# Collecting a mixture of experts' rows: block 0 summed by TensorE, the other tiles by VectorE alone, tables cleared at the start

## The chip, the cores and the metric

One core of one Trainium2 chip runs the whole program: a network of four layers on 4096 tokens of 128 features, float32 throughout. The metric is the device time of one run, in microseconds (us). A run of the kernel before takes 4406.22 us (median of three: 4403.34, 4406.22, 4411.11).

The engines by the names of the profile: PE is TensorE (matrix products), PEld its weight loads, DVE is VectorE, ACT is ScalarE, POOL is GpSimd, SP is SyncE, which only issues DMAs here. "L1742" is line 1742 of the kernel.

## The reference, cut to what matters

Each layer is a feed-forward, an attention, and the same feed-forward again. The change is in layer 3's feed-forward, which runs twice: before layer 3's attention and after it, as the last stage of the program. It is a mixture of 64 experts of which each token takes 8, with 64 places per expert, and one shared expert:

```python
probs = softmax(x @ router_w.T)
topk_w, topk_ids = top_k(probs, 8)            # 8 experts of 64 per token
topk_w = topk_w / sum(topk_w)
pos = place of the token among those that chose the expert, in token order
valid = pos < 64                              # C = 64 places per expert
y = (silu(xb @ w_gate) * (xb @ w_up)) @ w_down     # per expert, 64 rows each
routed = segment_sum(y[its 8 places] * weight * valid, token)
shared = silu(x @ ws_gate) * (x @ ws_up) @ ws_down
x = x + 0.5 * (routed + shared)               # on layernorm(x) as input
```

Places are given in token order over all 4096 tokens, so 64 experts with 64 places take 4096 of the 32768 choices: the first ones. Tokens late in the order get nothing from the experts.

## The kernel before

**Tiling.** x stays on chip as 32 tiles of 128 tokens; four tiles are a block (8 blocks). Tile and block lie in `self.X`; `self.XT` holds the normalized blocks with features on the partitions. A tile framework schedules the instructions of each engine from a model when the program is built, places the buffers of pools in memory, and inserts semaphore waits; each engine then executes its own list in order. DMAs stand in the list of the engine that issues them (SP, ACT or POOL) and wait there.

**Routing** (`ffn3`, L1709; `route`, L1744). `SOON = 3`: first only blocks 0 to 2 are routed. Per block, `stats` issues two DMAs that write zeros to 1 MB each of `parts` in DRAM (`clear`, L1738, issued by ACT at L1742; six in all) and takes the layer norm's moments, whose power -0.5 POOL forms (L168); `norm` scales (L175); `turn` transposes the block on PE (L185) and ACT copies it to XT (L187); `logits` multiplies (L1762) and DVE forms maximum (L1768) and difference (L1770), ACT the exponential (L1771); `choose` normalizes (L1777 to L1779), takes the eight largest (L1783, L1784), writes the row with its weights to `table` in DRAM (L1794, SP) and makes keys (L1800 to L1807). Five steps of three blocks are staggered (`route_blocks`, L1821). The keys are transposed (L1818, L1819), each expert's first 64 tokens are picked by eight rounds of "eight largest" (`choose_tokens`, L1843, L1845), and `places` makes a list of rows to fetch and of rows of `parts` to write. If some expert still has room, `more` is 1 and blocks 3 to 7 are routed too (`If`, L1892). In the profiled run `more` is 0: only 24 collecting reads (two times 12) are in the trace.

**Experts** (L1957). Eight groups of eight experts: POOL fetches the tokens' rows by indirect DMAs (L1951), PE multiplies, DVE weights the results, POOL scatters them by indirect DMAs to `parts` (L1988), where each token has eight rows of 128 numbers, one per chosen expert, zero where it got no place. The shared expert (L1912 to L1930) is interleaved.

**Collecting** (L2009 to L2029). For each of the 12 tiles of blocks 0 to 2: SP reads its eight rows per token, 512 KB, from `parts` (L2012, six buffers `co`); POOL adds the upper four rows to the lower four (128 partitions x 512, L2017); DVE halves the rest twice (128x256, L2018; 128x128, L2019) and adds half of the sum to x (L2021). Then `If(more)` (L2027) does the same for the other 20 tiles. An `If` is a branch on every engine; its other arm on SP waits until the DMA semaphores have reached the counts that they should have there, and adds what the skipped DMAs would have added. In the last call each block is stored by ACT when its four tiles are done (L2032).

**What follows the first call**: `attention3` (L804). It opens a pool, clears two value buffers V of 128x2048 (L827, POOL) and two of maxima (L831, POOL), normalizes block 0 (L164, L165, L167 on DVE, L168 on POOL, L175 on DVE), transposes it on PE (L975), copies it by ACT (L976) and forms queries and keys (L847, L849, L855, L857). L895 and L901 are its products and their maxima.

**The start of the program** (`ready2`, L2043): a zero tile `blank`; SP writes zeros with it to `table` (L2057, L2058), to `table2` for layer 2 (L2063, 16 DMAs of 1 MB) and to parts of `rel_rows` of layer 0's attention (L393).

## Time and profile before

| what | us |
|---|---|
| median of three runs | 4406.22 |
| the profiled execution | 4419.59 |
| its span, first to last instruction | 4417.8 |
| first routing, until the first fetch | 3437.7 to 3499.6 |
| first collecting, first read to the last sum | 3589.30 to 3621.77 |
| layer 3's attention, first scaling | 3622.38 |
| second routing, until the first fetch | 4230.7 to 4288.73 |
| second collecting, first read to the last sum | 4386.40 to 4413.49 |

| engine | busy us | share of the span |
|---|---|---|
| PE | 3785.8 | 86% |
| PEld | 2065.0 | 47% |
| DVE | 2765.6 | 63% |
| ACT | 2086.6 | 47% |
| POOL | 980.7 | 22% |

How to read it. The timeline gives instructions in order of start: start us, duration us, engine, line, operation, out<-in, count; in square brackets the engine's idle time before it and what ended it. "ACTq" or "SPq" is the issuing of a DMA in that engine's list, "POOLq" a wait there. The stretches give, for a part of the span, each engine's busy time with its number of instructions, the TensorE clock granted (1.00 is full speed), the share of the DMA engines' time and GB/s.

### The profile page before, as it was taken

The page shows a single profiled execution, that of the slowest core. Times are in us where ns is not written, and L with a number is a line of the kernel's source. Part 1 is how long each engine was busy: PE and PEld are TensorE (multiplying, and loading weights), DVE is VectorE, ACT ScalarE, POOL GpSimd, SP SyncE. Part 2 cuts the span into 40 slices and gives each one's busy share as a digit, 9 for nine tenths or more (in the row PEclk, how much of TensorE's full clock was granted, in tenths as well). Part 3 has the DMA queues.
Part 4 walks back from the last instruction along what each step waited for, and adds up shares of the span by engine and source line. Part 5 has one row for each costly group of instructions (what it writes and reads, how often), then busy time and mean ns, then how long its engine had stood idle before and what let it go on. Part 6 is the DMA issues. An engine that isn't in the chain of part 4 may idle for free. (4 is left out here: it accounts for less than half of the span.)

```text
span 4417.8 us, 64316 instructions
## 1 busy us (share of the span) xinstructions
PE 3785.8 (86%) x23046; PEld 2065.0 (47%) x23046; DVE 2765.6 (63%) x7495; ACT 2086.6 (47%) x4422; POOL 980.7 (22%) x1270
## 2 busy tenths in 40 slices
PE   8999999999999868899999967868667359999946
PEld 3445666666544345434344444467347233333324
DVE  5655777777756566656656466656553556777654
ACT  2335877878533324377877623312213015555521
POOL 1001111111000265211111266143024350000026
PEclk9999999999999979989999979969668579999967
DMA  6006777777300000000000000035007430000035
GB/s 256 0 5 203 220 226 221 223 221 225 93 1 1 5 0 1 1 1 1 1 1 1 1 0 2 8 100 172 0 13 239 153 125 1 1 1 1 1 109 169
DMA packets 217613, 331.79 MB, mean 75 GB/s; under 512 B 19954, under 2 KB 188380, under 8 KB 213700
## 3 DMA queue, kind: packets, MB, share of 16 engines
q1 hardware_dynamic: 197284, 290.59, 20.5%
q0 software_dynamic: 9664, 19.84, 1.5%
q10 hardware_dynamic: 10336, 17.17, 1.0%
q8 instruction: 183, 3.00, 0.3%
q14 instruction: 146, 1.20, 0.1%
HBM read 182.71 MB, written 144.82 MB: 74 GB/s over the span
## 5 line engine op out<-in xcount | busy, mean ns | idle before, releaser
L509 DVE CUSTOM_DVE_ANT_0 ps_s<-ps_s,PB 128x512 f32<-128x512 f32 x512 | 352.3, 704 | 155.5 <-PE ps_s L501 73.8
L901 DVE TENSOR_REDUCE nm<-ps_one 128x1 f32<-128x512 f32 x512 | 328.9, 685 | 155.4 <-PE ps_one L895 140.3
L513 ACT ACTIVATE pn<-ps_s,nm 128x512 f32<-128x512 f32 x512 | 356.8, 697 | 104.8 <-DVE nm L509 104.8
L907 ACT ACTIVATE pt<-ps_one 128x512 f32<-128x512 f32 x512 | 277.6, 595 | 203.7 <-PE ps_one L895 157.8
L168 POOL TENSOR_TENSOR ln_rs<-ln_rs,mhalf 128x4 f32<-128x4 f32 x128 | 132.7, 1037 | 897.5 <-DVE ln_rs L167 887.4
L895 PE MATMUL ps_one<-KT,QT 32*128 32x512 f32 x1024 | 307.5, 662 | 0.8 <-ACT KT L857 0.8
L675 ACT ACTIVATE sc<-sc,nm 128x512 f32<-128x512 f32 (+3 forms) x512 | 285.8, 562 | 39.5 <-DVE nm L732 33.3
L525 PE MATMUL ps_one<-ident,pn 128*128 128x128 f32 x2048 | 293.3, 282 | 12.2 <-DVE y L562 9.8
L732 DVE CUSTOM_DVE_ANT_0 sc<-ps_one,mask 128x512 f32<-128x512 f32 (+3 forms) x512 | 232.3, 487 | 105.5 <-PE ps_one L723 86.3
L887 PE MATMUL ps_one<-Q,KT 32*128 32x512 f32 x1024 | 289.7, 639 | 0.0
L326 ACT ACTIVATE sg<-ps_big 128x512 f32<-128x512 f32 x224 | 132.3, 597 | 320.2 <-PE ps_big L324 300.0
L450 PE MATMUL ps_one<-rdiff,QT 32*128 32x256 f32 x940 | 267.4, 404 | 14.5 <-ACT pt L528 14.4
L525 PEld LDWEIGHTS ps_one<-ident,pn 128*128 128x128 f32 x2048 | 219.1, 141 | 122.2 <-ACT pn L513 37.4
L327 DVE TENSOR_TENSOR sg<-sg,ps_big 128x512 f32<-128x512 f32 x224 | 152.3, 684 | 194.1 <-ACT sg L326 192.4
L739 ACT ACTIVATE pt<-ps_one 128x512 f32<-128x512 f32 (+3 forms) x512 | 209.6, 431 | 101.0 <-PE ps_one L723 92.9
L323 PE MATMUL ps_big<-XT,slot_a 128*128 128x512 f32 x448 | 236.7, 610 | 12.2 <-DVE sg L327 12.2
L501 PE MATMUL ps_s<-KT,QT 32*128 32x512 f32 (+2 forms) x1024 | 237.3, 540 | 0.8 <-ACT E L454 0.7
L324 PE MATMUL ps_big<-XT,slot_a 128*128 128x512 f32 x448 | 233.2, 602 | 0.0
L723 PE MATMUL ps_one<-KT,QT 32*128 32x512 f32 (+3 forms) x1024 | 229.7, 494 | 3.5 <-ACT pt L739 2.8
L715 PE MATMUL ps_one<-Q,KT 32*128 32x512 f32 (+3 forms) x1024 | 226.2, 483 | 6.8 <-ACT KT L662 5.8
L335 PE MATMUL ps_acc<-h,slot_a 128*128 128x512 f32 x448 | 229.8, 596 | 0.4 <-DVE h L329 0.4
L456 POOL COPY E<-E 128x127 f32<-128x127 f32 (+1 forms) x256 | 88.6, 346 | 637.2 <-ACT E L454 631.5
(436 smaller groups left out, 8386.1 us busy)
## 6 DMA issues: line engine op xcount, KB each, us to landing
rel_rows<-E SPq DMA_DIRECT2D x192, 383.0 KB, 3.7
PB<-rel_rows SPq DMA_DIRECT2D x128, 384.0 KB, 3.4
wt<-in_f_w_dram SPq DMA_DIRECT2D x78, 512.0 KB, 4.2
PB<-rel_rows SPq DMA_DIRECT2D x128, 256.0 KB
table<-blank SPq DMA_DIRECT2D x16, 1032.0 KB, 17.8
rel_rows<-E SPq DMA_DIRECT2D x64, 256.0 KB, 3.2
parts<-zero ACTq DMA_DIRECT2D x12, 1024.0 KB, 11.7
co<-parts SPq DMA_DIRECT2D x24, 512.0 KB, 7.1
```

Source lines behind the costliest of these rows:

```text
L323: nc.tensor.matmul(out=gu[:, 0, :], lhsT=w["f0_g"][:, cs], rhs=self.XT[:, b, :], start=True, stop=True)
L324: nc.tensor.matmul(out=gu[:, 1, :], lhsT=w["f0_u"][:, cs], rhs=self.XT[:, b, :], start=True, stop=True)
L450: nc.tensor.matmul(out=ps[:, c * 256 : c * 256 + 256], lhsT=Q[u][rr, i * P : (i + 1) * P], rhs=rdiff[rr, :], start=True, stop=True, tile_p ...
L501: nc.tensor.matmul(out=s[:, k, far:BT], lhsT=qt[rr, i * P : (i + 1) * P], rhs=kt[rr, far:BT], start=True, stop=True, tile_position=(32 * g ...
L509: nc.vector.tensor_tensor_reduce(out=s[:, k, :], in0=s[:, k, :], in1=pb[:, k, PB_AT[i] : PB_AT[i] + BT], scale=-1.0, scalar=1e30, op0=ALU. ...
L513: nc.scalar.activation(pn[:, k, :], s[:, k, :], AF.Exp, bias=nm[:, k : k + 1], scale=-1.0)
L525: nc.tensor.transpose(ps[:, j * P : (j + 1) * P], pn[:, k, j * P : (j + 1) * P], self.ident)
L675: nc.scalar.activation(sc[:, k, 0:wd], sc[:, k, 0:wd], AF.Exp, bias=maxs[u % 2][:, i, g, HD : HD + 1], scale=-1.0, accum_out=SUMS[u][:, i, ...
L887: nc.tensor.matmul(out=tw[k], lhsT=K[uw][rr, j * P : (j + 1) * P], rhs=Q2[uw][rr, :], start=True, stop=True, tile_position=(32 * g, 0),)
L895: nc.tensor.matmul(out=ts[k], lhsT=Q[u][rr, i * P : (i + 1) * P], rhs=K[u][rr, :], start=True, stop=True, tile_position=(32 * g, 0),)
L901: nc.vector.tensor_reduce(maxs[u % 2][:, i, 2 * hp + k : 2 * hp + k + 1, HD], ts[k], AX.X, ALU.max, negate=True)
L907: nc.scalar.activation(PT[m][:, k, :], tw[k], AF.Exp)
```

## The change

- `parts` is no longer one buffer, taken in each call and cleared there, but two buffers, one for each call, taken in `ready2`. The zeros of blocks 0 to 2 of both are written there by 12 DMAs of 1 MB on SP's queue, between those of `table` and those of `table2`. `clear(b)` remains for blocks 3 to 7 only.
- The collecting pool `f3c` is opened with `side="right"`.
- For a tile, DVE makes all three halvings (128x512, 128x256, 128x128); POOL does nothing.
- Block 0 is collected as a whole: four reads into one buffer `co4`, eight matmuls of 128x512 with the identity as weights that accumulate in PSUM, the k-th over row k of each of the 512 tokens, and one DVE instruction 128x512 that adds half of it to x.
- The order is now `If(more)`, block 0, tiles 4 to 11; before it was tiles 0 to 11, `If(more)`.

```diff
             table = self.table
-            parts = self.dram.tile([ROWS + NTOK, D], F32, name="parts", tag="parts", bufs=1)
+            parts = self.parts[last]
...
                 def stats():
-                    clear(b)
+                    if b >= SOON:
+                        clear(b)
                     box["mv"] = self.stats(self.tiles(b))
...
-        with self.tc.tile_pool(name="f3c", bufs=2) as pool:
+        with self.tc.tile_pool(name="f3c", bufs=2, side="right") as pool:
+            def read(dst, t):
+                nc.sync.dma_start(
+                    out=dst, in_=parts[t * P * K3 : (t + 1) * P * K3, :].rearrange("(p j) d -> p (j d)", j=K3)
+                )
+
             def collect(t):
                 c = pool.tile([P, K3, D], F32, name="co", tag="co", bufs=6)
-                nc.sync.dma_start(
-                    out=c.rearrange("p j d -> p (j d)"),
-                    in_=parts[t * P * K3 : (t + 1) * P * K3, :].rearrange("(p j) d -> p (j d)", j=K3),
-                )
+                read(c.rearrange("p j d -> p (j d)"), t)
                 r = pool.tile([P, 4, D], F32, name="cr", tag="cr")
-                nc.gpsimd.tensor_tensor(out=r, in0=c[:, 0:4, :], in1=c[:, 4:8, :], op=ALU.add)
-                nc.vector.tensor_tensor(r[:, 0:2, :], r[:, 0:2, :], r[:, 2:4, :], ALU.add)
-                nc.vector.tensor_tensor(r[:, 0, :], r[:, 0, :], r[:, 1, :], ALU.add)
+                for n in (4, 2, 1):
+                    src = c if n == 4 else r
+                    nc.vector.tensor_tensor(r[:, 0:n, :], src[:, 0:n, :], src[:, n : 2 * n, :], ALU.add)
                 x = self.X[:, t, :]
                 nc.vector.scalar_tensor_tensor(x, r[:, 0, :], 0.5, x, ALU.mult, ALU.add)
...
-            for t in range(4 * SOON):
-                collect(t)
+            def collect_block(b):
+
+                c = pool.tile([P, 4, K3 * D], F32, name="co4", bufs=1)
+                for j in range(4):
+                    read(c[:, j, :], 4 * b + j)
+                ps = self.mid()
+                for k in range(K3):
+                    nc.tensor.matmul(
+                        out=ps.rearrange("p (j d) -> p j d", d=D), lhsT=self.ident,
+                        rhs=c[:, :, k * D : (k + 1) * D], start=(k == 0), stop=(k == K3 - 1),
+                    )
+                x = self.xblk(b).rearrange("p j d -> p (j d)")
+                nc.vector.scalar_tensor_tensor(x, ps, 0.5, x, ALU.mult, ALU.add)
+                if last:
+                    self.store(b)
+
             with self.tc.If(more):
                 for t in range(4 * SOON, NT):
                     collect(t)
+            collect_block(0)
+            for t in range(4, 4 * SOON):
+                collect(t)
...
         nc.sync.dma_start(out=self.table[NTOK : NTOK + 1, :], in_=rows[0:1, 0, :])
+
+        self.parts = [
+            self.dram.tile([9 * NTOK, D], F32, name="parts%d" % n, tag="parts%d" % n, bufs=1) for n in range(2)
+        ]
+        for n in range(2 * self.SOON):
+            for p in self.parts:
+                nc.sync.dma_start(
+                    out=p[n * 16 * P : (n + 1) * 16 * P, :].rearrange("(p k) c -> p (k c)", k=16), in_=zero[:, 0 : 16 * D]
+                )
```

More of the change, by code (lines that the diff above doesn't have):

```diff
@@ L1706, in attn2 @@
                 nc.vector.tensor_tensor(x, x, po, ALU.add)
+    SOON = 3
     def ffn3(self, last):
@@ L1717, in ffn3 @@
         HALF = NTOK // 2
-        SOON = 3
+        SOON = self.SOON
         with self.tc.tile_pool(name="f3", bufs=1) as pool, self.tc.tile_pool(name="f3b", bufs=2) as pool2:
             table = self.table
-            parts = self.dram.tile([ROWS + NTOK, D], F32, name="parts", tag="parts", bufs=1)
+            parts = self.parts[last]
             zero = pool.tile([P, 16 * D], F32, name="zero")
```

## The prediction

> **What bounds the kernel now.** Layer 3's feed-forward runs twice and takes about 317 us of the 4417.8; nothing outside it is edited, except twelve DMA issues at the start. I read first the stretches of both calls (routing, collecting, start of the attention), then the timeline inside each, then the waits, then the order of instructions in the changed program with the semaphores that each waits for.

> The stretches (us; then busy time and instructions of PE, PEld, DVE, ACT, POOL; granted clock; DMA share; GB/s):

> ```profile
> 3430.00:3500.00 70.00, 12.22 (x47) 8.74 (x47) 50.31 (x180) 3.75 (x8) 10.34 (x12) 0.50 0.44 160
> ...
> 3588.00:3622.00 34.00, 0.00 (x0) 0.00 (x0) 24.13 (x56) 0.00 (x0) 17.22 (x14) 0.50 0.50 187
> 3622.00:3660.00 38.00, 33.21 (x78) 11.06 (x82) 23.56 (x55) 3.66 (x6) 7.02 (x8) 0.51 0.00 0
> ```

> Routing and collecting are DVE's: PE does nothing in the collecting. So what counts is when DVE starts, what holds it up, and how fast PE's next work comes free. Routing of the first call:

> ```profile
> 3436.91 0.69 DVE L1612 TENSOR_TENSOR X<-X,yg 128x512 f32<-128x512 f32 x1 [0.80 <-DMA yg<-f_y]
> ...
> 3441.30 0.59 ACT L187 COPY XT<-ps_mid 128x512 f32<-128x512 f32 x1 [22.80 <-PE ps_mid L185]
> 3441.93 10.72 ACTq L1742 DMA_DIRECT2D parts<-zero  x6
> ...
> 3444.87 0.85 DVE L175 TENSOR_SCALAR xw<-X,ln_mv,ln_rs 128x128 f32<-128x128 f32 x3
> 3452.70 0.42 ACT L1771 ACTIVATE p<-p 128x256 f32<-128x256 f32 x1 [10.82 <-DMA parts<-zero]
> 3453.03 0.57 ACT L187 COPY XT<-ps_mid 128x512 f32<-128x512 f32 x1
> 3453.15 0.42 DVE L1777 TENSOR_REDUCE r_s<-p 128x4 f32<-128x256 f32 x1 [7.43 <-ACT p L1771]
> ```

> The reader is to see that six DMA issues stand in ACT's list ahead of block 0's exponential; DVE, ready at 3445.72, waits 7.43 us. In the second call the same six cost DVE 3.51 us (L1777 starts at 4243.24). In the collecting:

> ```profile
> 4399.13 1.32 POOL L2017 TENSOR_TENSOR cr<-co 128x512 f32<-128x512 f32 x1 [0.61 <-DVE X L2021]
> 4399.37 1.23 DVE L2019 TENSOR_TENSOR cr<-cr 128x128 f32<-128x128 f32 x1
> 4400.64 0.29 DVE L2021 SCALAR_TENSOR_TENSOR X<-cr,X 128x128 f32<-128x128 f32 x1
> 4400.85 0.42 DVE L2018 TENSOR_TENSOR cr<-cr 128x256 f32<-128x256 f32 x1
> 4401.06 1.32 POOL L2017 TENSOR_TENSOR cr<-co 128x512 f32<-128x512 f32 x1 [0.61 <-DVE X L2021]
> ```

> A tile takes 1.93 us, and DVE's 128x128 add, 0.29 us alone, lasts 1.23 us while POOL's add runs. Last, the handover to the attention:

> ```profile
> 3621.48 0.29 DVE L2021 SCALAR_TENSOR_TENSOR X<-cr,X 128x128 f32<-128x128 f32 x1
> 3622.11 3.69 POOL L827 MEMSET V<- 128x2048 f32 x2 [2.26 <-DVEq L2027]
> 3622.38 3.57 DVE L175 TENSOR_SCALAR xn<-X,ln_mv,ln_rs 128x128 f32<-128x128 f32 x4 [0.61 <-DVEq L2027]
> ...
> 3626.72 0.58 ACT L976 COPY XT<-ps_one 128x512 f32<-128x512 f32 x1 [45.28 <-PE ps_one L975]
> ```

> **The change, part by part.**

> *Clears out of the calls.* In the changed list ACT does block 0's copy, block 1's copy, then block 0's exponential. First call: block 1's transposes end at 3444.76, its copy about 3445.4, the exponential about 3445.7, so L1777 starts about 3445.75: 7.4 us earlier. DVE's list is also rearranged: block 1's maximum (L1768) is now second, and waits for logits that PE forms from 3445.4 for 1.97 us: a new wait of 1.2 us, with all of DVE's routing queued behind it. The old wait of 0.89 us for block 2's logits shrinks to about 0.1. Net 7.4 - 1.2 + 0.8 = **7.0 us**. Second call: block 0's differences are ready at 4239.73, L1777 moves from 4243.24 to 4240.2, 3.04 - 1.2 + 0.8 = **2.6 us**. From there to the fetches all is DVE work in a row, so the shift arrives whole.

> *Clears at the start.* Twelve issues and 12.6 MB on SP's queue ahead of table2's. The DMA engines are saturated (402 to 422 GB/s) until 78 us, then idle (2 GB/s or less) until the first transfer of layer 0's attention at 329.06 us; 12.6 MB at 410 GB/s is 31 us, ending about 109 us. Everything queued behind on SP shifts by as much: table2 and rel_rows zeros, needed 220 us later. Cost 0; had the cover been gone, 31 us.

> *Collecting, first call.* Let R be the first read's issue (3589.30, last scatter landed); both programs wait for the same scatters. Reads move 408 to 422 GB/s, 1.27 us each. The first is used at R+3.4; by the bytes moved, the fifth lands at R+8.4. In the changed list DVE does tiles 4 to 8, then block 0's addition, then tiles 9 to 11. A tile: the 128x512 add is not in this stage before; L1612 (above, two inputs on chip) takes 0.69. With 0.45, 0.33 and 0.21 between the starts that follow, 1.71 us. It could not beat POOL's 1.93 by more than 0.5, nor be worse than 0.69 replaced by 1.25. PE's eight matmuls: a 128x512 float32 one takes 0.85 between starts at clock 0.50 (L855), so 6.8 us, from R+7 to R+15 with all reads in; hidden, since DVE asks for them only at R+17. Sum: 8.4 + 5 x 1.71 + 0.65 + 3 x 1.6 + 1.1 for the interleaved statistics of the attention = R+23.5; before R+32.5. The 9 us do not all arrive. In the changed program V's clearing waits for DVE's semaphore at the last tile's sum, so the right-hand pool does not free the attention of it, and the power for block 0's norm (L168), which before stood among the collecting additions, now stands behind the clearings in POOL's list: 0.15 + 3.69 + 1.3 for the small ones + 1.03 = R+29.7. Then four scalings of 0.28, a transpose, and the copy (L976) at R+31.5; before R+37.4. Gain **5.9 us**. Were V not held, DVE's statistics would be next and the copy about R+27: 4.5 more.

> *Collecting, second call.* Here the scheduler has put block 0's first read ahead of the `If`, whose other arm on SP waits for that read to land. A read alone: 3.24 us (the chain's first "co<-parts" piece). So the other eleven leave at R+3.9; tile 4, fourth of them, lands at about R+10.9 instead of R+8.4. PE then ends near R+17, still under the tiles. 10.9 + 8 x 1.71 + 0.65 = R+25.3 against R+27.1: gain **1.8 us** (4.3 if the wait cost nothing; -0.5 if the tiles took 2.0 each). The store of the last block stands behind it as before. The `If` was off the tail already (0.61 us on DVE in the first call, beside a store here).

> Sum: 7.0 + 2.6 + 5.9 + 1.8 = 17.3 us. The profiled execution took 4419.59 (4417.8 and 1.8 around it), so that one would be 4402.3; it lay 13.4 above the median of the runs, and I carry the difference to the median: 4406.22 - 17.3 = **4389 us**.

> [...] From 3622 to 3660 PE is busy 33.21 of 38 us, at clock 0.51. [...]

> **Rivals.**

> [...]
> 2. *Slower: half clock for longer.* [...] From 3660 to 4230 PE is busy 562.92 of 570 us, so each us more at half clock costs about 0.5. To end 0.2% above before, it must lose 26 us, 52 us more of it: 4415 and above. Nothing but chance speaks for it.
> 3. *Only the fronts.* Reads land later than by the bytes, or the 128x512 add costs more, and both tails give nothing: 9.6 us, 4396.6. For: 1.71 is put together from rows of other places.
> 4. *Better tails.* V's clearing or the second call's reads hold up less than counted: 7 us more, 4382.
> 5. *It does not do what it says* is in part sure (the pool still holds V) and counted.

> **How the numbers follow.** Forecast 60% (4384 to 4395, its own terms' bounds); rival 1 8%, rival 2 5%, rival 3 15%, rival 4 12%. The range 4379 to 4399 takes in the forecast, 3 and 4. About 0.2%, 8.8 us, is what a measurement can tell from no change, so faster is below 4397.4: 60 + 12 + 8 and half of rival 3, 87%; same 9%; slower 4%.

> **What would show it.** Right: block 0's exponential about 0.4 us after block 1's copy, DVE's wait before block 1's maximum about 1.2 us in both calls; no POOL additions in the collecting and DVE's 128x128 adds at 0.29; block 0's addition waiting for nothing; POOL's power behind the clearings and the copy L976 about 31.5 us after the first read; in the second call a gap of 3 to 4 us on SP between the first and second read. Wrong: DVE idle before tile 5 or later (reads bind), PE's sums later than tile 8, the stretch at half clock much longer or shorter than 36 us, or layer 0's attention starting later than before.

## The result and the profile after

The changed kernel takes 4400.62 us (median of 20 runs, 4390.15 to 4406.53); the kernel before, run beside it, 4408.32 us (20 runs, 4398.92 to 4418.63). The ratio is 0.9979, 95% interval 0.9972 to 0.9986. So it is faster, by 7.7 us between the medians (9.9 between the means), where 17.3 were forecast. Two later pairs, on other chips, gave 0.9973 (0.9959 to 0.9986) and 0.9989 (0.9978 to 0.9999).

The profiled execution of the changed kernel has a span of 4403.2 us against 4417.8: 14.6 less. That is twice the difference of the medians, and it is the riddle of this case. First the stretches of the changed kernel, with the same columns as before the change:

```profile
3430.00:3500.00 70.00, 13.65 (x50) 9.30 (x50) 54.01 (x199) 3.87 (x8) 14.58 (x16) 0.50 0.25 75
...
3588.00:3622.00 34.00, 16.63 (x32) 6.81 (x34) 21.97 (x79) 1.96 (x3) 8.75 (x10) 0.60 0.38 151
3622.00:3660.00 38.00, 38.00 (x143) 12.42 (x137) 24.02 (x41) 10.33 (x17) 0.00 (x0) 0.65 0.00 0
```

Everything has moved forward: PE, idle in the collecting before, now has 16.63 us of work between 3588 and 3622 (the sums of block 0, then the attention's start), and the attention fills the stretch from 3622. The clock column is 0.50 to 0.65. Stretch by stretch, with two traces of each kernel (the second pair is of a chip on which both traces are some 54 us longer: some 42 of it ahead of the attention's first queries, 13 to 14 in the second call's experts, whose rows go by indirect DMAs, and none of it in the stretches of the table):

| stretch, us | before | after | before, 2nd | after, 2nd |
|---|---|---|---|---|
| first routing, first constant (L1731, L1733) to first fetch | 61.90 | 55.52 | 61.62 | 55.50 |
| first collecting, first read to the attention's first copy (L976) | 37.42 | 31.52 | 37.59 | 31.82 |
| attention, that copy to the last addition to X (L960) | 604.6 | 604.6 | 602.1 | 604.7 |
| second routing, first constant to first fetch | 57.48 | 57.06 | 58.03 | 56.92 |
| second collecting, first read to the end of the span | 31.40 | 29.97 | 31.39 | 29.08 |

The four edited stretches give 6.4 + 5.9 + 0.4 + 1.4 = 14.1 us in the first pair and 6.1 + 5.8 + 1.1 + 2.3 = 15.3 in the second. The first front, in the changed kernel's timeline (L1774 is the exponential, L1780 the sum behind it, L1771 a block's maximum):

```profile
3445.79 0.59 ACT L187 COPY XT<-ps_mid 128x512 f32<-128x512 f32 x1 [2.91 <-PE ps_mid L185]
...
3446.47 0.42 ACT L1774 ACTIVATE p<-p 128x256 f32<-128x256 f32 x1
3446.92 0.42 DVE L1780 TENSOR_REDUCE r_s<-p 128x4 f32<-128x256 f32 x1 [0.20 <-ACT p L1774]
```

ACT goes from block 1's copy straight to the exponential, and the sum waits 0.20 us where it waited 7.43. The second front, where little was gained, first two rows of the kernel before, then the changed kernel:

```profile
4243.24 0.42 DVE L1777 TENSOR_REDUCE r_s<-p 128x4 f32<-128x256 f32 x1 [3.51 <-ACT p L1771]
...
4249.24 0.42 DVE L1768 TENSOR_REDUCE r_nm<-ps_mid 128x4 f32<-128x256 f32 x1 [0.89 <-PE ps_mid L1762]
```

```profile
4230.77 0.59 ACT L187 COPY XT<-ps_mid 128x512 f32<-128x512 f32 x1 [2.60 <-PE ps_mid L185]
...
4233.42 0.42 DVE L1771 TENSOR_REDUCE r_nm<-ps_mid 128x4 f32<-128x256 f32 x1 [2.28 <-PE ps_mid L1765]
4233.76 0.34 DVE L1786 MAX8 r_m<-p 128x8 f32<-128x64 f32 x2
```

DVE stands 2.28 us before block 2's maximum, where it stood 0.89; block 0's choice (MAX8) has all it needs, but is queued behind it. Collecting and handover:

```profile
3600.30 0.68 DVE L2024 TENSOR_TENSOR cr<-co 128x512 f32<-128x512 f32 x1
...
3601.02 0.75 DVE L2024 TENSOR_TENSOR cr<-cr 128x256 f32<-128x256 f32 x2
3601.81 0.29 DVE L2026 SCALAR_TENSOR_TENSOR X<-cr,X 128x128 f32<-128x128 f32 x1
3602.02 0.68 DVE L2042 SCALAR_TENSOR_TENSOR X<-ps_mid,X 128x512 f32<-128x512 f32 x1
...
3607.63 3.57 POOL L827 MEMSET V<- 128x2048 f32 x2 [25.83 <-DVE ln_mv L165]
...
3608.03 1.43 DVE L167 TENSOR_SCALAR ln_rs<-ln_mv 128x4 f32<-128x4 f32 x1
...
3612.34 2.02 POOL L168 TENSOR_TENSOR ln_rs<-ln_rs,mhalf 128x4 f32<-128x4 f32 x2
3613.41 1.12 DVE L175 TENSOR_SCALAR xn<-X,ln_mv,ln_rs 128x128 f32<-128x128 f32 x4 [2.19 <-POOL ln_rs L168]
...
3615.15 0.59 ACT L976 COPY XT<-ps_one 128x512 f32<-128x512 f32 x1 [39.74 <-PE ps_one L975]
```

A tile takes 1.72 us (3600.30 to 3602.02), block 0's addition (L2042) waits for nothing (by little, see below), and the norm's power (L168) stands behind the clearings, as forecast.

### The profile page after: what moved, and what is told of

The parts are those of the page before. It is cut to its first block, busy times and chain, and to the rows that moved or that the text cites. A ratio compares the mean times of both kernels' runs of the same rounds, so it can differ in the third digit from the quotient of the medians.

```text
span 4403.2 us, 64326 instructions
## 1 busy us (share of the span) xinstructions
PE 3800.1 (86%) x23078; PEld 2070.6 (47%) x23078; DVE 2748.3 (62%) x7489; ACT 2088.1 (47%) x4422; POOL 952.1 (22%) x1246
## 5 line engine op out<-in xcount | busy, mean ns | idle before, releaser
L168 POOL TENSOR_TENSOR ln_rs<-ln_rs,mhalf 128x4 f32<-128x4 f32 x128 | 132.5, 1036 | 898.9 <-DVE ln_rs L167 888.8
L895 PE MATMUL ps_one<-KT,QT 32*128 32x512 f32 x1024 | 307.9, 663 | 0.8 <-ACT KT L857 0.8
L450 PE MATMUL ps_one<-rdiff,QT 32*128 32x256 f32 x940 | 267.1, 403 | 14.6 <-ACT pt L528 14.5
L525 PEld LDWEIGHTS ps_one<-ident,pn 128*128 128x128 f32 x2048 | 219.0, 141 | 122.5 <-ACT pn L513 37.4
## 6 DMA issues: line engine op xcount, KB each, us to landing
parts<-blank SPq DMA_DIRECT2D x12, 1024.0 KB, 14.1
```

Source lines behind the costliest of these rows:

```text
L450: nc.tensor.matmul(out=ps[:, c * 256 : c * 256 + 256], lhsT=Q[u][rr, i * P : (i + 1) * P], rhs=rdiff[rr, :], start=True, stop=True, tile_p ...
L525: nc.tensor.transpose(ps[:, j * P : (j + 1) * P], pn[:, k, j * P : (j + 1) * P], self.ident)
L895: nc.tensor.matmul(out=ts[k], lhsT=Q[u][rr, i * P : (i + 1) * P], rhs=K[u][rr, :], start=True, stop=True, tile_position=(32 * g, 0),)
```

## The experiments

Each kernel is the changed one with one edit unless said otherwise. "Attention" is always the time from its first copy to the last addition to X.

**1. Second traces, and each half alone.** `clears` is the kernel before with the early clears, `collect` the kernel before with the new collecting.

> The kernel before, unchanged: a second trace of it. The traces of the first pair of executions differ by 14.6 us (4417.8 and 4403.2), the medians by 7.7. Theory A (terms right, this kernel's typical execution has shorter stalls than the profiled one): the first call's wait of VectorE for block 0's exponential, 7.43 us in the first trace, or the collecting (37.4 us from its first read to the attention's first copy) comes out some us shorter here. Theory B (clock): those stretches are the same to 0.3 us, and what differs is how long TensorE stays at half clock after the collecting (33.0 us from that copy in the first trace), in steps of some us. Time 1.000 of itself.

> The changed kernel, unchanged: a second trace. Theory A: its stretches are those of the first trace to 0.3 us (front 55.5 us from the first key constant to the first fetch, 31.5 from the first read to the attention's copy) and only the kernel before varies. Theory B: the stretches agree too, but the time at half clock behind the collecting (34.0 us in the first trace) is longer here, 40 to 55. Ratio 0.998 again by both.

> The kernel before with the early clears and the two tables alone, collecting as it was. By the terms of the first pair of traces 6.4 us in the first call's front, 0.4 in the second's and about 1 behind: ratio 0.9982. Theory A with shorter typical stalls: 2 to 4 us, 0.9993. Theory B: the stretches shrink by 6 to 8 us and the median moves by that less what the clock gives or takes, either sign, up to 7.

> The kernel before with the changed collecting alone (block 0 by TensorE, other tiles by VectorE, pool at the other end), the clears left in the calls. By the first pair of traces 5.9 us in the first call and 1.4 in the second: ratio 0.9983. Theory A (the collecting of typical executions is shorter than in the profiled one): 0.9993. Theory B: first read to the attention's copy 31.5 us as in the changed kernel, and a time at half clock behind it that differs by several us from the 33.0 of before; ratio 0.9983 plus or minus 0.0015.

Measured, on the slower chip (kernel before 4464.75 us in 35 runs): the kernel before against itself 1.0000 (0.9986 to 1.0014), the changed kernel 0.9973 (0.9959 to 0.9986), clears 0.9983 (0.9971 to 0.9995), collect 0.9987 (0.9976 to 0.9999). The stretches repeat to 0.9 us, those of the halves too (first front 55.57 with clears, first read to copy 31.65 with collect): theory A falls, the first trace's waits were the usual ones. What differs between executions is the half clock after the attention's first copy: 26, 34, 33 and 26 us in the four traces. Theory B stood in its main point, without saying why; the 40 to 55 us that it expected of the changed kernel were 34.

**2. Keep PE busy until the attention; three edits of the change's own losses.**

```diff
 # warm                                   # iflast: the If behind the tiles
+for k in range(26):                       collect_block(0)
+    nc.tensor.matmul(out=warm, ...)       for t in range(4, 4 * SOON): collect(t)
                                           with self.tc.If(more): ...
 # order: maximum kept in the probabilities' buffer (bufs=2)
-nm = self.sm([P, 4], "r_nm")
+nm = pm[:, 4 * NE3 :]
 # vlate: clearings written behind block 0's norm
+at(-7, blanks)
```

> The changed kernel, with 26 idle products of block 0's rows (128x512, result unused) behind block 0's sum in the first call, so that TensorE has work from the sum until the attention's first transpose. It tests the half clock at the attention's start, 33 to 34 us in the changed kernel and 33 or 26 in the kernel before; where it was 26 the attention as a whole took 2.5 us less (602.1 against 604.6 from its first copy), 0.3 us for each us. Theory: the stretch is a state left by the idle collecting; kept busy, the attention starts at clock 1.00 and ends 9 to 11 us sooner. [...] The collecting itself must not move: 31.5 us from first read to the attention's copy, 32 if the last idle product is late.

> The changed kernel, with the maximum kept in the same buffer as the probabilities (two buffers), so that VectorE forms block 2's maximum only when block 0 is done. In the changed kernel's second call VectorE stands 2.27 us before block 2's maximum, which waits for logits that TensorE and ScalarE deliver every 3.50 us per block, while block 0's choice is queued behind it. Theory: this is where the forecast 2.6 us of the second front went; second front 57.0 to about 54.9 us, first front unchanged (55.5, within 0.5). Rival: the front is bound by that chain anyway, and the time comes back at block 2: 56.5 to 57.

> The changed kernel, with the branch behind the twelve tiles, as in the kernel before. Theory: in the changed kernel's second call the first read stands ahead of the branch and the other eleven wait for it to land, 3 us; without it tile 4 lands 2.5 to 3 us sooner and the span ends 26.5 to 27 us after the first read, where it was 30.0 and 29.1. Rival: the reads were hidden behind the tiles, 29 us. In the first call the attention's statistics can no longer mix with the tiles; from first read to the attention's copy 31.5 to 33.

> The changed kernel, with the clearing of the attention's value buffers written behind block 0's norm; the build places one of the two big clearings ahead of the norm's power on GpSimd and one behind it. Theory: the power, which starts 28.7 us after the first read in the changed kernel though its moments are there 2.5 us earlier, starts at about 26, and the attention's copy comes 28.7 to 29.2 us after the first read, 31.5 before; the span is shorter by that, 2.5 us. Rival: VectorE's moments, stretched beside the clearing (1.4 us for what takes 0.2 to 0.5 alone), are the limit, and it stays at 31.

`warm` failed as an experiment, and taught something: each product is two PE instructions of 0.43 us at full clock, so the 26 took 22.5 us, the attention came 14 us late (first read to copy 45.46 us, span 4414.4), and still started at half clock for 34 us: the clock, 1.00 until 3626.54, fell behind the one window with gaps between the idle products and the attention's first (PE busy 0.63 of 3.41 us). `order` shortened the second front from 57.06 to 54.60 us: the 2.3 us were the wait, not a bound. `iflast` shortened the second collecting to 28.10 us (29.97 and 29.08 in the changed kernel's traces; 26.5 to 27 expected). One row each shows why, SP's twelve reads in the changed kernel and in iflast:

```profile
4373.23 15.51 SPq L2014 DMA_DIRECT2D co<-parts  x12
```

```profile
4361.60 13.37 SPq L2014 DMA_DIRECT2D co<-parts  x12
```

`vlate` gained nothing (copy 31.72 us after the first read). Its timeline shows the rival's reason:

```profile
3610.60 1.04 POOL L168 TENSOR_TENSOR ln_rs<-ln_rs,mhalf 128x4 f32<-128x4 f32 x1 [0.17 <-DVE ln_st L164]
3611.61 1.79 POOL L830 MEMSET V<- 128x2048 f32 x1
3611.67 3.53 DVE L175 TENSOR_SCALAR xn<-X,ln_mv,ln_rs 128x128 f32<-128x128 f32 x4
```

The power came sooner, but the second clearing then ran beside DVE's four scalings, which took 3.53 us instead of 1.12.

The surprise was in `order` and `iflast`: their attention took 593.4 and 593.3 us, 9 to 11 less than in any trace so far, with the clock up within 4 us of the copy. Neither edit touches the attention's code. I call a start with the clock up so soon warm, and one that stays at half clock for 26 to 34 us cold. The clock changes at points of a grid 3.41 us apart: in the first pair of traces all 74 and 78 stretches of one clock begin on such a grid, and so lie the 56 to 66 changes followed in each of four later traces (after_third, delay and the two looks of experiment 4). It need not change at each, and the grid's place differs from execution to execution: counted from the span's start it is offset by 0.1 us in the first trace of the changed kernel, by 3.1 in vlate's. So I laid the windows between these points over the timelines; at the attention's start they hold one clock each, 0.50 or 1.00, in all 18 traces. The changed kernel (columns as above):

```profile
3611.36:3614.77 3.41, 0.91 (x4) 0.73 (x4) 1.32 (x6) 0.00 (x0) 3.00 (x6) 0.50 0.00 0
3614.77:3618.18 3.41, 2.68 (x5) 1.18 (x4) 3.41 (x21) 0.81 (x2) 1.01 (x1) 0.50 0.01 2
3618.18:3621.60 3.42, 2.64 (x10) 0.75 (x10) 0.06 (x1) 1.15 (x2) 1.01 (x1) 0.50 0.00 0
3621.60:3625.01 3.41, 3.41 (x12) 1.17 (x10) 2.55 (x5) 0.00 (x0) 0.00 (x0) 0.50 0.00 0
```

And `order`:

```profile
3609.18:3612.59 3.41, 1.20 (x4) 0.73 (x4) 1.81 (x9) 0.10 (x1) 2.52 (x4) 0.50 0.00 0
3612.59:3616.01 3.42, 2.89 (x4) 1.18 (x4) 2.98 (x19) 1.17 (x2) 1.49 (x2) 0.50 0.01 2
3616.01:3619.42 3.41, 2.63 (x15) 0.90 (x14) 0.96 (x2) 0.69 (x1) 0.52 (x1) 1.00 0.00 0
```

The attention's first two products, one of queries (L847) and one of keys (L855), two PE instructions each, use all 128 rows and last 3.9 us at half clock. In `order` one window holds 2.89 us of PE work, mostly theirs, and the clock is 1.00 from the next; in the changed kernel it holds 2.68, the clock stays, and the later windows, full (3.41) but with products of 32 rows between, did not lift it for another 20 to 30 us.

**3. Take the lot out.** `dense` forms the second group's queries and keys right behind the first's; `before_dense` is the kernel before with this edit; `vearly` opens a pool for the attention's value buffers and clears them ahead of the collecting; `best` has dense, order, iflast and vearly.

```diff
-at(8 * u - 5, lambda u=u: queries(u))
-at(8 * u - 3, lambda u=u: keys(u))
+at(-2 if u == 1 else 8 * u - 5, lambda u=u: queries(u))
+at(-2 if u == 1 else 8 * u - 3, lambda u=u: keys(u))
 # vearly, ahead of the collecting's pool, first call
+pool = self.held.enter_context(self.tc.tile_pool(name="v3", bufs=1))
+self.vals = [pool.tile(...) ...]; for v in self.vals: nc.gpsimd.memset(v, 0.0) ...
```

> The changed kernel, with the queries and keys of the attention's second group formed right behind those of the first, so that four products of 128x512 with 128 rows stand in a row, 7.7 us at half clock where two took 3.9. In the ten traces so far the attention's first block of products starts 0.34 and 0.53 us behind a change point of the clock (these lie 3.41 us apart) where the clock came up within 4 us (attention 593.3 and 593.4 us), and 0.82 to 2.10 us behind one where it stayed at half for 26 to 34 us (602.1 to 604.7). Theory: the clock comes up when one such 3.41 us window is nearly filled (2.9 of 3.41 us was enough, 2.7 not) by products that use all rows; 7.7 us always fill one, so the attention takes 593 to 596 us in every execution, and the executions scatter less (5.2 us standard deviation of the changed kernel before, 3 to 4 here). Rival: the start of the attention is not what decides, and this kernel scatters as before, with 604 us in some traces.

> The kernel before with the same single edit of the attention. Theory: with the clock's lot taken out of both, the change is worth what its stretches show, 14.6 us (6.2 first front, 5.8 first collecting, 0.8 second front, 1.8 second collecting): the medians of this one and of the kernel with the edit and the change differ by 12.5 to 16.5 us. Rival: if the change really is worth only the 8 to 10 us between the first medians, they differ by that here too.

> The changed kernel, with the attention's value buffers and maxima in a pool of their own that is opened and cleared before the collecting, so that nothing is left to clear behind it. With half of the clearing moved behind the norm's power, the power started 2.7 us sooner but VectorE's four scalings beside the clearing took 3.53 us where they take 1.12 alone, and the copy came 31.7 us after the first read all the same. Theory: with no clearing there, moments, power and scalings follow one another, copy at 26.5 to 27.5 us after the first read (31.5 before): 4 to 5 us. Rival: the clearing at the collecting's start slows the first tiles or waits for the pool, copy at 29 or later.

> Everything that helped: the changed kernel with the branch last, block 2's maximum held back, value buffers cleared before the collecting, four dense products at the attention's start. Theory, against the kernel with the dense start alone: second front 2.4 us, first collecting 4 to 5, second collecting 1.5: 8 to 9 us; against the kernel before some 30 us where that starts its attention at half clock and some 20 where not: ratio 0.9935 to 0.9955. Rival: the edits hinder one another (the statistics behind the branch instead of between the tiles): 4 us less.

Measured (kernel before 4408.08 us in 15 runs): dense 4392.2 us (5 runs, 4391.1 to 4396.1; ratio 0.9964, 0.9951 to 0.9978), before_dense 4407.5 us (11 runs; 0.9995, 0.9986 to 1.0004). The two differ by 15.3 us by the medians and 14.7 by the means, what the stretches give; the rival's 8 to 10 are out. Dense's times lie where the changed kernel's lower group lies (4390.2 to 4395.9 in the first 20 runs). The attention took 597.0, 593.8 and 593.7 us in dense, before_dense and best. So the lot is not wholly out: the four products lifted the clock in all three traces, but in dense's it fell again behind a window filled mostly by products of 32 rows (L895):

```profile
3615.08:3618.49 3.41, 3.41 (x17) 1.18 (x15) 1.11 (x2) 1.37 (x2) 0.00 (x0) 1.00 0.00 0
3618.49:3621.91 3.42, 3.42 (x15) 1.65 (x15) 3.42 (x8) 0.00 (x0) 0.00 (x0) 1.00 0.00 0
3621.91:3625.32 3.41, 3.41 (x14) 1.58 (x10) 3.41 (x7) 0.00 (x0) 0.00 (x0) 0.50 0.00 0
```

It stayed at half for 13.7 us, and one of before_dense's eleven runs took 4414.6 us. `vearly` copies 27.71 us after the first read (31.5 in the changed kernel, 26.5 to 27.5 expected):

```profile
3579.68 3.55 POOL L2011 MEMSET V<- 128x2048 f32 x2 [1.57 <-DMA parts<-y,dest]
...
3604.84 1.04 POOL L168 TENSOR_TENSOR ln_rs<-ln_rs,mhalf 128x4 f32<-128x4 f32 x1 [20.46 <-DVE ln_rs L167]
3605.91 1.11 DVE L175 TENSOR_SCALAR xn<-X,ln_mv,ln_rs 128x128 f32<-128x128 f32 x4 [0.77 <-POOL ln_rs L168]
```

POOL clears before the first tile is there, and power and scalings follow one another. `best` takes 4386.05 us (5 runs, 4380.0 to 4388.1), ratio 0.9941 (0.9928 to 0.9955): the fastest version, 22 us below the kernel before; against dense 6.2 us by the medians and 9.0 by the means, forecast 8 to 9.

**4. Later, and faster?** `delay` makes block 0's copy five times; beside it the changed kernel again and two more traces of the kernel before.

```diff
-nc.scalar.copy(self.XT[:, b, :], ps)
+for _ in range(5 if b == 0 else 1):
+    nc.scalar.copy(self.XT[:, b, :], ps)
```

> The changed kernel made later on purpose: block 0's copy for the attention is made five times instead of once, 2.3 us more before its first queries, nothing else. In the changed kernel's two traces these start 1.02 and 0.82 us behind a change point of the clock, and both stayed at half for 34 us; 2.3 us more puts them 3.1 us behind one, that is 0.3 before the next, where the products fill the following window. Theory: the clock comes up at once in most executions, 11.2 us less for 2.3 us more; the median lies 3 to 8 us below that of the changed kernel on the same chip, although work was added, and the trace shows 593 to 594 us from the last copy to the attention's end. Rival: the place in the window is not the cause; the median rises by 2.3 us.

> The changed kernel, unchanged, beside the delayed one on the same chip. Theory: most executions start the attention at half clock for 34 us (12 of the first 20 times lie at 4400 to 4407, 8 at 4390 to 4396), median about 4400 where the kernel before takes 4408.

> The kernel before, one more trace. With the attention's start made dense, the kernel before gained only 1.4 us in the mean, the changed one about 6. Theory: most executions of the kernel before start the attention warm, and its two traces with 33 and 26 us at half clock were of the rarer kind; here the attention takes 593 us from its first copy and the span is 4404 to 4407 on a chip of 4408 us. Rival: it starts cold in nearly all, 602 to 605 us.

> As the look before: 593 us by the theory in most looks, 602 to 605 by the rival.

On a chip where the kernel before takes 4404.94 us (23 runs), delay took 4397.41 us (12 runs; 0.9983, 0.9972 to 0.9993), the changed kernel 4402.76 (12 runs; 0.9989, 0.9978 to 0.9999). The median is 5.4 us lower with 2.5 us of work added, as the theory wants; but the means differ by 2.1 us only, with a standard error of 2.3, and five of delay's twelve times still lie at 4403 to 4407. This run alone does not settle it. The traces do: delay's came up at once (593.4 us from the last copy), and the kernel before started warm in both traces, here in the first of them (columns as above):

```profile
3623.83:3627.24 3.41, 1.64 (x3) 0.79 (x4) 3.38 (x15) 0.59 (x1) 2.21 (x5) 0.50 0.00 0
3627.24:3630.65 3.41, 2.83 (x4) 0.68 (x2) 1.43 (x10) 1.23 (x2) 2.03 (x2) 0.50 0.00 0
3630.65:3634.07 3.42, 3.22 (x18) 1.53 (x18) 1.99 (x4) 0.15 (x1) 0.00 (x0) 1.00 0.01 2
```

The middle window holds 2.83 us of work, and the next has the full clock. All traces without the dense start, by how far behind a point of the grid the first queries begin:

| queries begin, us behind a grid point | kernels | attention, us |
|---|---|---|
| 0.09 (delay), 0.35 (iflast), 0.53 (order) | changed | 593.3 to 593.4 |
| 0.82, 0.88, 1.02 (changed kernel, three traces), 0.91 (vearly), 1.09 (warm) | changed | 604.5 to 604.7 |
| 2.10 (vlate) | changed | 604.5 |
| 1.74 (clears), 2.11 (before) | old collecting | 604.3, 604.6 |
| 2.01 (before), 2.03 (collect) | either | 602.1 |
| 2.47, 2.80 (before, two traces) | old collecting | 592.9 |

So it was at this place in the program in every trace: where one window held 2.83 us or more of this block's work, the clock came up at its end; with 2.69 or less it did not.

## Why the prediction was right and wrong

- **First front, 7.0 forecast, 6.4 and 6.1 measured.** Right; the exponential starts right behind block 1's copy, as written, and the new wait ahead of block 1's maximum is 1.10 us (1.2 forecast).
- **Second front, 2.6 forecast, 0.4 and 1.1 measured. This step failed.** I wrote that "the old wait of 0.89 us for block 2's logits shrinks to about 0.1". Once the clears are gone, the chain of PE and ACT at half clock, one block each 3.50 us, is late next, and DVE's new list puts block 2's maximum ahead of block 0's choice: the wait became 2.28 us. `order`, which holds that maximum back, won 2.5 us. Two smaller terms were off as well: counted from the first constant, the sum behind the exponential starts 2.1 us sooner, not 3.0 (block 1's scalings, which wait 1.20 us for POOL's power, now stand ahead of it), and the new wait ahead of block 1's maximum, 1.2 us by the forecast, is none in this call.
- **Early clears, nothing forecast.** Right: layer 0's first queries are formed at 324.04 us, 323.94 before.
- **First collecting, 5.9 forecast, 5.9 and 5.8 measured**, the copy 31.52 us after the first read where R+31.5 was forecast. Two terms inside were off and covered: the first tile's addition began at R+9.8 instead of R+8.4, and PE's eight products took 10.0 us, not 6.8 (each is two PE instructions; I had read one). They ended at R+18.2, and DVE asked for them at R+18.4. That they stayed hidden was luck: in the changed kernel's three traces they ended 0.05 to 0.14 us before DVE asked, because the clock rose to 1.00 midway (at 3597.70 in the first). At half clock throughout, 16 instructions at 0.85 us would take 13.6 us and end some 3.5 us late (an estimate).
- **Second collecting, 1.8 forecast, 1.4 and 2.3 measured.** Right by the span; by the last sum, which the forecast counted (R+25.3 against R+27.1), it came at R+26.4 and R+25.6, a gain of 0.7 and 1.6, and the other 0.7 us came behind it, between the last sum and the end of the span (4.28 us before, 3.55 after), where none was forecast. The cause was right: SP's second read leaves 3.6 us behind the first, and its list is 3 us longer than in the first call (15.51 against 12.56 us); `iflast` took back 1 to 2 us.
- **From the stretches to the median. This is the step that failed.** The sum for the stretches, 17.3, was 2.7 too high. The rest was lost here: "it lay 13.4 above the median of the runs, and I carry the difference to the median". That difference was no constant. The profiled execution was of the cold kind (attention 604.6 us), and the kernel before starts warm (592.9) in two of its four traces; the changed kernel started cold in all three of its traces. If the upper group of times is the cold one (4400 and above in 13 of the changed kernel's first 20 runs, 4416 and above in 4 of 20 before), the change gave back 0.45 x 11.2 = 5.0 us of its 14.6; that leaves 9.6, and the means differ by 9.9. That the groups of times are these two kinds is argued, not shown run by run. Three things bear it out. Two traces of the kernel before, 4417.8 and 4405.9 us long, start every indirect DMA ahead of the attention within 2.1 us of one another, and 12 to 13 us apart behind it. The granted clock that is on record for each run goes with its time (changed kernel, first 20 runs: 0.909 to 0.912 in the seven below 4396 us, 0.906 to 0.909 in the thirteen above 4400), though it does not say where in the program the half clock lay. And with the dense start in both kernels the medians lie the full 15.3 us apart.
- **The rivals.** Rival 1, at 8%, was an attention that starts warm, worth at most half of the 33.21 us that PE works between 3622 and 3660, 16 us; rival 2, at 5%, was half clock for longer. I thought them two opposite accidents. They are the two faces of one lot that each execution draws, worth 11.2 us, and the change has shifted the odds. I had not asked where between two points of the clock's grid the attention's first products begin; the table above shows how the attention's time goes with it. "Nothing but chance speaks for it" was truer than meant. Rival 3, only the fronts, names a gain of 9.6 us, near the measured one, for the wrong reason: both tails gave what was forecast.

What stays open: why the start falls so regularly near 0.9 us behind a change point in the changed kernel and near 2.0 to 2.8 in the kernel before, though the grid's offset differs from trace to trace (0.1 to 3.1 us from the span's start); earlier stages that end at half clock may tie the program to it, which is a guess that was not tried. Open too is what it is in a product that lifts the clock (last section).

## What to carry to other kernels

Before a difference is carried from one profiled execution to a median, look whether that execution is of the usual kind: compare its clock's stretches in two or three traces, and lay 3.41 us windows over the place where PE starts after a pause. Where an engine's stall is removed, follow the next chain with its own pace (here 3.50 us per block at half clock) and read the changed order of the list for work queued behind a new wait. Where a start should be warm, put a block of dense products there rather than trust a lucky place: four in a row (7.7 us at half clock, by the 3.9 of two) lifted the clock in all three traces that have them (dense, before_dense, best), though in dense's it fell back later.

## What the runs showed of the hardware

```profile
2560.05:2563.46 3.41, 2.98 (x5) 1.24 (x5) 3.17 (x5) 1.84 (x5) 0.00 (x0) 0.50 0.00 0
2563.46:2566.88 3.42, 1.89 (x3) 0.44 (x2) 2.90 (x5) 0.53 (x2) 0.99 (x1) 0.50 0.00 0
```

- Four DVE scalings of 128x128 with operands per partition take 1.12 us alone and 3.53 us beside POOL's clearing of 128x2048; a 128x4 one 0.15 and 1.43.
- The same program took 4405, 4408 or 4465 us (medians) by the chip; of the 54 us more in the traces of the slowest, some 42 lie ahead of the attention's first queries and 13 to 14 in the second call's experts, whose rows go by indirect DMAs.
